# A shared root chain for two normalisations, the first tokens' normalisation on another engine, and four more unused products, in an RWKV and mixture-of-experts kernel

## The chip, the cores and the metric

The kernel runs on one core of one Trainium2 chip. A core has a matrix engine (TensorE, PE in the profile; its weight loads are listed as PEld), VectorE (DVE), ScalarE (ACT), GpSimd (POOL) and SyncE (SP), which issues most transfers. Each engine works through its own queue in order; semaphores tie the queues together. The metric is the device time of one execution in microseconds (us): the median of several runs.

## The reference, cut to what matters

Two blocks follow each other, each with a normalisation in front of it and a residual sum behind it. `x` has 4 sequences of 1024 tokens with 256 channels; everything is float32.

```python
def _layernorm(x, axis=-1, eps=1e-05):
    m = jnp.mean(x, axis=axis, keepdims=True)
    v = jnp.var(x, axis=axis, keepdims=True)
    return (x - m) / jnp.sqrt(v + eps)
...
# attention (RWKV), on the normalised tokens
xx = jnp.pad(x, ((0, 0), (1, 0), (0, 0)))[:, :Tv] - x
xk = x + xx * time_maa_k            # likewise xv, xr, xg
r, k, v = xr @ Wr.T, xk @ Wk.T, xv @ Wv.T
g = jax.nn.gelu(xg @ Wg.T, approximate=False)
def step(state, inp):
    rc, kc, vc = inp
    att = rc @ kc
    yc = att * Wmat @ vc + rc @ state * wb
    new_state = ws * state + kc * wk @ vc
    return (new_state, yc)
# y is normalised per head, then: out = yn * g @ Wo.T
...
# experts, on the tokens normalised again: 8 experts, the best 2 of each token, capacity 320
h1 = jnp.einsum('ebcm,emh->ebch', dispatch, w1)
h3 = jnp.einsum('ebcm,emh->ebch', dispatch, w3)
expert_out = jnp.einsum('ebch,ehm->ebcm', jax.nn.silu(h1) * h3, w2)
```

So every token is normalised twice: once ahead of the attention, and once, after the attention's output has been added, ahead of the experts.

## The kernel before, in words

**Blocks.** The 4096 tokens are worked in 16 blocks of 256 tokens (two tiles of 128), four to a sequence. The tokens lie in SBUF in rows of 512 tokens (`RT` = 4 tiles), so a row holds two blocks. For a block, `front` (L375) normalises the tokens (`xn`, by `normed`, L367), transposes them on PE (`trx`, L398), copies them out (`xT`, L401), takes the difference to the token before (`xx`, L405 on DVE for the first block, L407 on POOL for the others), mixes (`xm`, L413) and multiplies by the weights (`pc`, L423; `pt`, L464). `chunk` (L492) does the recurrence for one tile: scores `pa` (L502), their decay weights `aw` on DVE (L510), the outputs `y` (L524, L531) and the update of the state `pu` (L543) and `upd` (L550). `back` (L564) normalises per head (`sq`, `ys`, `var`, roots in `rsqrt`, `prs`), multiplies by the output weights (`po`, L610) and adds to the tokens (L615).

**Normalisation.** `norm_stats` (L329) works on one row: for each of its four tiles ACT sums the tokens (L347) and their squared deviations (L350), each followed by a read of the accumulator, and then DVE scales the variances (L354), takes their inverse roots by a bit trick and two steps of iteration (`rsqrt`, L308: ten small instructions, L317 to L325) and multiplies (L359). It is called with a key `a` ahead of the attention and with a key `f` in `logits` (L621) ahead of the experts. A call is a generator: each `yield` hands back to the loop, which decides when the next part is recorded. For the first 256 tokens the statistics are taken on DVE (`by_rows`, L337) and those of the other half of that row on ACT, behind the eight diagonals (L251, `last_diag`). `normed` is an ACT instruction for all tokens.

**Experts.** `logits` and `route` choose the experts and scatter the tokens to a buffer in HBM (L815) in five segments; `expert` (L850) loads weights and tokens, multiplies (`p`, L915, and `pw`, L936), and adds the results to the output by an indirect transfer (L943). These products fill PE between those of the attention.

**Order.** PE's order is written out by hand: the loop over blocks (L1091) goes through 15 stages, and in each it advances the parts listed for it (`f` and `fa` the fronts of later blocks, `c` the chunks, `bk` and `new` the backs, `st` the statistics), then `routing` by two steps, and then as many expert products as a credit allows (`RATES`). Experts of a segment may start `LAGS` stages after its routing is done. The queues of the other engines are set by a scheduler from the same record; `tc.issue_after(ins)` asks that what is recorded in its block comes behind `ins`. Until the change, the statistics of block n + 2 are taken in block n when n is even, and `f` statistics of a row one block after its second half.

**The start.** Ahead of the loop stand the first statistics, 18 products of ones with ones whose result nobody reads (`warm`, L1045), the statistics of the second half row, the first two fronts, and the decay tables: 16 instructions `wmat` (L257) on ACT, which need `lam`, which ACT computes (L222) and DVE clamps (L223).

```python
    with tc.issue_after(last["first_xn"]):
        decay_of_heads(0)
    with tc.issue_after(first_copy):
        decay_of_heads(1)
        decay_of_keys()
```

`first_xn` is the second of the two `xn` instructions of the first block (L386), kept in program order (L385).

Of the kernel before, what the change touches and what calls it, by code (L numbers as in the profile page):

```python
# [9 lines left out]
F32 = mybir.dt.float32  # L10
I32 = mybir.dt.int32
AF = mybir.ActivationFunctionType
ALU = mybir.AluOpType
# [4 lines left out]
P = 128  # L18
B, T, C = 4, 1024, 256
# [5 lines left out]
TPB = TB // P  # L25
BPS = T // TB
RB = 512
RT = RB // P
RPS = T // RB
# [11 lines left out]
AFTER = (0, 2, 3, 4)  # L41
# [5 lines left out]
LN_EPS = 1e-5  # L47
# [7 lines left out]

LAGS = (8, 5, 4, 4)

WARM = 18

SCORES = (0, 6)  # L60
MAGIC = 0x5F3759DF
ROOT = (64.0 / 9.0) ** 2
# [3 lines left out]
def rwkv_then_moe_kernel(  # L66
# [12 lines left out]
    nc = tc.nc  # L79
# [5 lines left out]
    sm = ctx.enter_context(tc.tile_pool(name="sm", bufs=1))  # L85
# [18 lines left out]
    xb = {}  # L104
# [203 lines left out]
    def rsqrt(v, n, nm):  # L308
# [17 lines left out]

        return y, (guess, lambda: step(9.0 / 64.0))

    def norm_stats(key, src, nm, t0=0, n=RT, behind=None, by_rows=False):  # L329

        ve = sm.tile([P, n], F32, tag=f"ve{n}", name=f"ve{nm}", bufs=2)
        nb = sm.tile([P, n], F32, tag=f"nb{n}", name=f"nb{nm}", bufs=2)
        if by_rows:
            st = sm.tile([P, n, 6], F32, tag="st", name=f"st{nm}", bufs=2)
            mv = sm.tile([P, n, 2], F32, tag="mv", name=f"mv{nm}", bufs=2)
            for t in range(n):
                nc.vector.bn_stats(st[:, t, :], src[:, t0 + t, :])  # L337
                nc.vector.bn_aggr(mv[:, t, :], st[:, t, :])
                yield
            mean, sign = mv[:, :, 0], -1.0  # L340
            nc.vector.tensor_scalar(ve, mv[:, :, 1], LN_EPS, ROOT, ALU.add, ALU.mult)
        else:

            mean, sign = sm.tile([P, n], F32, tag="mn", name=f"mn{nm}", bufs=2), 1.0
            for t in range(n):
                with tc.issue_after(behind) if behind else nullcontext():
                    nc.scalar.activation(  # L347
                        aside, src[:, t0 + t, :], AF.Copy, scale=-1.0 / C,
                        accum_out=mean[:, t:t + 1])
                nc.scalar.activation(  # L350
                    aside, src[:, t0 + t, :], AF.Square, bias=mean[:, t:t + 1],
                    accum_out=ve[:, t:t + 1])
                yield
            nc.vector.tensor_scalar(ve, ve, ROOT / C, LN_EPS * ROOT, ALU.mult, ALU.add)  # L354
        rs, parts = rsqrt(ve, n, nm)
        parts[0]()
        yield
        parts[1]()
        last["nb"] = nc.vector.scalar_tensor_tensor(  # L359
            nb, mean, sign, rs, ALU.mult, ALU.mult).ins  # L360
        stats[key] = rs, nb, t0

    stats = {}

    aside = const.tile([P, C], F32, tag="aside", name="aside")

    def normed(dst, src, key, t):  # L367
        rs, nb, t0 = stats[key]
        t -= t0
        return nc.scalar.activation(  # L370
            dst, src, AF.Identity, bias=nb[:, t:t + 1], scale=rs[:, t:t + 1])
# [249 lines left out]
    def logits(b, r):  # L621

        nm = f"{b}_{r}"
        nc.sync.dma_start(out=rows(out, b, r), in_=xb[b, r])
        yield from norm_stats(("f", b, r), xb[b, r], f"f{nm}")
        yield
        hs = a2.tile([P, RT, W], F32, tag="hs", name=f"hs{nm}")
        nc.gpsimd.iota(
            hs.bitcast(I32)[:, :, C:C + 1], pattern=[[P, RT], [0, 1]], base=b * T + r * RB,
            channel_multiplier=1)  # L630
        for t in range(RT):
            normed(hs[:, t, :C], xb[b, r][:, t, :], ("f", b, r), t)
            if t == TPB - 1:
                yield
        g = segment_of(b, r)
        t0 = r * RT - SEGMENTS[g][1]
        if t0 == 0:
            last["hs"] = []
            last["lg"] = sm.tile([P, SEGMENTS[g][2], E], F32, tag="lg", name=f"lg{g}", bufs=2)
        last["hs"].append(hs)  # L640
        yield from (None,) * (6 if g < AFTER[1] else 2)

        hTs = []
        for u in range(RT // TPB):
            pt = bank("m", f"trh{nm}_{u}")
            for cc in range(CC):
                for i in range(TPB):
                    nc.tensor.transpose(
                        pt[:, cc * TB + i * P:cc * TB + (i + 1) * P],
                        hs[:, u * TPB + i, cc * P:(cc + 1) * P], ident)  # L650
            hT = a1.tile([P, CC, TB], F32, tag="hT", name=f"hT{nm}_{u}", bufs=2)
            nc.scalar.copy(hT.rearrange("p cc i -> p (cc i)"), pt)
            hTs.append(hT)
            yield
        yield from (None,) * 3
        pl = bank("m", f"pl{nm}")
        for cc in range(CC):
            for t in range(RT):
                u, i = divmod(t, TPB)
                nc.tensor.matmul(  # L660
                    pl[32 * t:32 * t + 32, :P], gt[:, cc, :], hTs[u][:, cc, i * P:(i + 1) * P],
                    start=cc == 0, stop=cc == CC - 1, tile_position=(0, 32 * t),
                    skip_group_check=True,
                )
        lgT = sm.tile([P, P], F32, tag="lgT", name=f"lgT{nm}")
        nc.scalar.copy(lgT, pl[:, :P])
        yield from (None,) * 3
        pg = bank("m", f"plt{nm}")
        nc.tensor.transpose(pg[:, :P], lgT, ident)
        nc.scalar.copy(  # L670
            last["lg"][:, t0:t0 + RT, :],
            pg[:, :P].rearrange("p (t e) -> p t e", t=RT)[:, :, :E])
        yield from (None,) * 2
# [416 lines left out]
    with tc.manual_schedule(engines={ENG.PE}):  # L1090
        for n in range(NBLK):  # L1091
            b, blk = divmod(n, BPS)
            f, (fa, after) = f1, fronts(n + 2)
            st = iter(())
            if n + 2 < NBLK and n % RPS == 0:
                sb, sblk = divmod(n + 2, BPS)
                sr = sblk * TPB // RT
                st = norm_stats(("a", sb, sr, 0), xb[sb, sr], f"a{sb}_{sblk}", behind=last["xm"])
            if blk % RPS == 0 and b + 1 < B:
                load_x(b + 1, blk // RPS)  # L1100
            if blk == 0:
                last["state"] = None
            c = [chunk(b, blk, t, cur) for t in range(TPB)]
            new = back(b, blk, cur)
            for i, stage in enumerate((
                (c[0], st),
                (f, st),
                (c[0], st),
                (bk, st),
                (f, bk, st),  # L1110
                (c[0], st),
                (c[1], fa, st),
                (f,),
                (fa, bk),
                (c[1],),
                (f,),
                (bk,),
                (f,),
                (c[1], fa, new),
                (),  # L1120
            )):
                for part in stage:
                    steps(part)
                steps(routing, 2)
                clock.step += 1
                credit = min(credit + RATES[clock.turn], 4 * RATES[clock.turn])

                drain = i in SCORES
                while credit > 0 or drain:
                    drain = False  # L1130
                    cols = next(work, None)
                    if cols is None:
                        break
                    credit -= cols
            if n and n * TPB % RT == 0:
                pb, pblk = divmod(n - 1, BPS)
                routing = chain(routing, routed(pb, pblk * TPB // RT))
            cur, nxt, f1, bk = nxt, after, fa, new

        clock.mixed = True  # L1140
        for _ in bk:
            next(work, None)
        for _ in chain(routing, routed(B - 1, RPS - 1)):
            clock.step += 1
            if clock.step % 2:
                next(work, None)
        clock.mixed = False

        over = sm.tile([P, E + 1], F32, tag="over", name="over")
        nc.vector.tensor_scalar_add(  # L1150
            over[:, :E], last["base"], -float((TILES[B - 1] + SURE) * P))
        nc.vector.tensor_reduce(over[:, E:], last["base"], AX.X, ALU.max)
        nc.vector.tensor_scalar_add(over[:, E:], over[:, E:], -float(TILES[B] * P))
        last["over"] = sm.tile([P, E + 1], I32, tag="overi", name="overi")
        nc.vector.tensor_copy(last["over"], over)
        for _ in work:
            clock.step += 1
# [44 lines left out]
```

## Time and profile before

| what | value |
|---|---|
| median of 3 runs | 989.05 us (988.8 to 991.5) |
| the profiled execution | 978.46 us |
| its span, first to last instruction | 976.7 us |
| PE busy | 944.2 us (97%) |
| PEld busy | 749.7 us (77%) |
| DVE busy | 447.0 us (46%) |
| ACT busy | 320.1 us (33%) |
| POOL busy | 244.6 us (25%) |
| mean granted clock of PE | 0.988 |

In a line of the timeline the columns are: start in us from the span's start, length in us, engine, line of the kernel, operation, output <- inputs, shapes and number of instructions merged in the line; in brackets stands how long the engine had been idle before it and what ended that wait. `x4` on PE counts passes: a float32 product of 128 by 256 takes two. PEclk is the clock that PE was granted, as a share of full speed. A line of groups ends with busy time, mean length of one instruction in ns, and the idle time before.

### The profile page before, as it was taken

Reading aid. Unit: us, or ns where it says so; the run is one execution under the profiler, and the core shown is the slowest. Engines: PE = TensorE matmul, PEld = TensorE weight load, DVE = VectorE, ACT = ScalarE, POOL = GpSimd, SP = SyncE. Lnnn points to the kernel's source line nnn. Section 1 sums busy time; section 2 is a strip of 40 time slices with the busy share of each in tenths; the row PEclk is TensorE's granted clock in tenths of the full one; section 3 lists DMA queues with packets and bytes.
Section 4 is the critical chain, followed back from the end, with each engine's and each line's share of the span. In section 5 each row is a group of like instructions: output and inputs, shape, how many; then the busy total and the mean of one; then the engine's idle time right before and its main releaser. Section 6 shows DMA issues by size and latency. Waiting matters only on the chain. (4 is left out here: it accounts for less than half of the span.)

```text
span 976.7 us, 17096 instructions
## 1 busy us (share of the span) xinstructions
PE 944.2 (97%) x6754; PEld 749.7 (77%) x6754; DVE 447.0 (46%) x1303; ACT 320.1 (33%) x811; POOL 244.6 (25%) x265
## 2 busy tenths in 40 slices
PE   7989899999999999999999999999999999999995
PEld 6766678878787788888788778888866866767664
DVE  7888766656676634445443434322221222222221
ACT  8647544743654531524214124111111111111110
POOL 5321513312227212121452111541111110211111
PEclk9999999989999999999999999999999999999998
DMA  5997224514446444353465545785645234433421
GB/s 162 245 252 244 84 95 142 184 60 141 153 125 219 153 124 136 93 153 89 128 192 151 153 135 157 208 248 168 175 123 153 76 87 147 135 94 92 147 54 19
DMA packets 92073, 139.06 MB, mean 142 GB/s; under 512 B 5456, under 2 KB 73552, under 8 KB 91984
## 3 DMA queue, kind: packets, MB, share of 16 engines
q1 hardware_dynamic: 79120, 120.36, 39.2%
q0 software_dynamic: 12720, 17.47, 9.7%
q8 instruction: 58, 0.95, 0.4%
q14 instruction: 31, 0.25, 0.1%
q10 hardware_dynamic: 144, 0.02, 0.0%
HBM read 103.45 MB, written 34.39 MB: 141 GB/s over the span
## 5 line engine op out<-in xcount | busy, mean ns | idle before, releaser
L915 PE MATMUL p<-xeT,w 128*128 128x256 f32 (+2 forms) x1960 | 430.8, 374 | 2.8 <-DVE act L904 1.5
L915 PEld LDWEIGHTS p<-xeT,w 128*128 128x128 f32 x1960 | 328.4, 191 | 94.8 <-issue 10.5
L920 ACT ACTIVATE sl<-p 128x256 f32<-128x256 f32 (+2 forms) x245 | 91.2, 375 | 486.6 <-PE p L915 479.1
L904 DVE TENSOR_TENSOR act<-sl,p 128x256 f32<-128x256 f32 (+2 forms) x245 | 99.5, 408 | 284.2 <-ACT sl L920 168.4
L943 POOL DMA_INDIRECT y_out<-ye,xe x67 | 105.3, 1571 | 478.0 <-DVE ye L940 448.1
L936 PE MATMUL pw<-w,act 128*128 128x256 f32 x938 | 211.9, 381 | 0.3 <-DVE act L904 0.3
L936 PEld LDWEIGHTS pw<-w,act 128*128 128x128 f32 x938 | 174.9, 190 | 24.6 <-DVE act L904 1.0
L940 DVE TENSOR_SCALAR ye<-pw,xe 128x256 f32<-128x256 f32 x67 | 32.1, 483 | 138.6 <-PE pw L936 138.5
L510 DVE TENSOR_TENSOR aw<-pa,wmat 128x512 f32<-128x512 f32 x128 | 79.4, 683 | 11.4 <-PE pa L502 11.3
L815 POOL DMA_INDIRECT disp<-hs,is x64 | 63.7, 996 | 44.3 <-issue 15.4
L423 PE MATMUL pc<-xm,wa 128*128 128x256 f32 x264 | 67.1, 400 | 5.9 <-DVE aw L510 3.1
L423 PEld LDWEIGHTS pc<-xm,wa 128*128 128x128 f32 x264 | 50.2, 198 | 16.2 <-DVE aw L510 3.7
L413 DVE SCALAR_TENSOR_TENSOR xm<-xx,ch,xT 128x256 f32<-128x256 f32 x98 | 43.5, 479 | 8.5 <-PE pc L423 5.1
L502 PE MATMUL pa<-rT,kT 32*128 32x256 f32 x512 | 43.1, 410 | 2.0 <-DVE rbT L443 1.1
L531 PE MATMUL y<-aw,vpad 128*32 128x128 f32 x1024 | 40.5, 278 | 0.0
L347 ACT ACTIVATE aside<-x 128x256 f32<-128x256 f32 x62 | 25.7, 415 | 37.8 <-DVE x L615 37.0
L502 PEld LDWEIGHTS pa<-rT,kT 32*128 32x128 f32 x512 | 26.5, 187 | 11.2 <-issue 3.4
L610 PE MATMUL po<-wa,zT 128*128 128x256 f32 x128 | 30.7, 383 | 4.1 <-DVE zT L602 2.6
L531 PEld LDWEIGHTS y<-aw,vpad 128*32 128x32 f32 x1024 | 24.4, 109 | 12.2 <-issue 11.7
L464 PE MATMUL pt<-wa,xm 128*128 128x256 f32 x128 | 32.2, 397 | 0.9 <-DVE rbT L443 0.9
L407 POOL TENSOR_TENSOR xx<-xT 128x512 f32<-128x512 f32 x15 | 15.7, 1049 | 67.2 <-ACT xT L401 67.2
L610 PEld LDWEIGHTS po<-wa,zT 128*128 128x128 f32 x128 | 23.5, 190 | 7.9 <-ACT xT L393 2.8
(184 smaller groups left out, 797.3 us busy)
## 6 DMA issues: line engine op xcount, KB each, us to landing
w<-w_in SPq DMA_DIRECT2D x96, 896.0 KB, 6.4
disp<-empty SPq DMA_DIRECT2D x8, 795.0 KB, 15.4
disp<-empty SPq DMA_DIRECT2D x16, 265.0 KB, 9.5
xe<-disp SPq DMA_DIRECT2D x16, 265.0 KB, 2.9
xe<-disp SPq DMA_DIRECT2D x8, 530.0 KB
y_out<-x SPq DMA_DIRECT2D x8, 512.0 KB, 3.3
x<-x_in SPq DMA_DIRECT2D x7, 512.0 KB, 4.3
wa<-w_attn_in SPq DMA_DIRECT2D x5, 256.0 KB, 4.9
```

The source lines that it names most:

```text
L413: last["xm"] = nc.vector.scalar_tensor_tensor(xm[:, cc, :], xx[:, cc, :], maa(m, cc), xT[:, cc, 1:TB + 1], ALU.mult, ALU.add,).ins
L423: nc.tensor.matmul(pp[:, m * TB:(m + 1) * TB], wa[w][:, cc, m * P:(m + 1) * P], xm[:, cc, :], start=cc == 0, stop=cc == CC - 1,)
L502: nc.tensor.matmul(pa[g][:, cc * TB:(cc + 1) * TB], o.kT[rows32, cc, cols], o.rT[rows32, cc, :, cols], start=True, stop=True, tile_positio ...
L510: nc.vector.tensor_tensor(w.rearrange("p q i -> p (q i)"), pa[g], wmat[:, 4 * g:4 * g + 4, :].rearrange("p q i -> p (q i)"), ALU.mult,)
L531: nc.tensor.matmul(y[32 * g:32 * g + 32, :], o.vp[:, t, cc * 4 + g, q * 32:(q + 1) * 32], aw[g][:, cc * 2 + q, :], start=state is None and ...
L610: nc.tensor.matmul(po[:, t * C:(t + 1) * C], zT[:, cc, t * P:(t + 1) * P], wa[W_O][:, cc, :], start=cc == 0, stop=cc == CC - 1,)
L815: ins = nc.gpsimd.indirect_dma_start(out=disp[:, :], out_offset=bass.IndirectOffsetOnAxis(ap=idx_s[g][:, c, t:t + 1], axis=0), in_=last["h ...
L904: nc.vector.tensor_tensor(act, sl, p3[:, :w], ALU.mult)
L915: nc.tensor.matmul(pp[:, :w], wt[:, cc, f * P:(f + 1) * P], xeT[:, cc, lo:lo + w], start=cc == 0, stop=cc == CC - 1,)
L920: nc.scalar.activation(sl, p1[:, :w], AF.Silu)
L936: nc.tensor.matmul(po[:, :C], acts[f][:, i * P:(i + 1) * P], w2e[:, f, :], start=f == 0, stop=f == FC - 1,)
L943: ins = nc.gpsimd.indirect_dma_start(out=out[:, :], out_offset=bass.IndirectOffsetOnAxis(ap=xe.bitcast(I32)[:, t, C:C + 1], axis=0), in_=y ...
```

## The change

It has four parts. `WARM` goes from 18 to 22. The `xn` of the first block become DVE instructions. A new generator, `norm_pair`, takes the statistics of two rows together, the `f` row of blocks n - 3 and n - 2 and the `a` row of block n + 3, and runs one root chain over eight columns; it is used in blocks 3, 5, 7, 9 and 11, and the `a` statistics are taken in odd blocks instead of even ones (in block 0 and block 1 still by `norm_stats`). `logits` waits ten empty steps for a row whose statistics come from a pair, and two empty steps fewer behind its `hs`, for the first segments.

```diff
-WARM = 18
+WARM = 22
...
+    def norm_pair(keys, srcs, nm, behind):
+
+        n = 2 * RT
+        mean = sm.tile([P, n], F32, tag="mn8", name=f"mn{nm}", bufs=2)
+        ve = sm.tile([P, n], F32, tag="ve8", name=f"ve{nm}", bufs=2)
+        nb = sm.tile([P, n], F32, tag="nb8", name=f"nb{nm}", bufs=2)
+        for i, src in enumerate(srcs):
+            for t in range(RT):
+                o = i * RT + t
+                with tc.issue_after(behind) if i else nullcontext():
+                    nc.scalar.activation(
+                        aside, src[:, t, :], AF.Copy, scale=-1.0 / C,
+                        accum_out=mean[:, o:o + 1])
+                nc.scalar.activation(
+                    aside, src[:, t, :], AF.Square, bias=mean[:, o:o + 1],
+                    accum_out=ve[:, o:o + 1])
+                if t % 2:
+                    yield
+        nc.vector.tensor_scalar(ve, ve, ROOT / C, LN_EPS * ROOT, ALU.mult, ALU.add)
+        rs, parts = rsqrt(ve, n, nm)
+        parts[0]()
+        yield
+        parts[1]()
+        nc.vector.tensor_tensor(nb, mean, rs, ALU.mult)
+        for i, key in enumerate(keys):
+            sl = slice(i * RT, (i + 1) * RT)
+            stats[key] = rs[:, sl], nb[:, sl], 0
...
     def normed(dst, src, key, t):
         rs, nb, t0 = stats[key]
+        if key == ("a", 0, 0, 0):
+            return nc.vector.tensor_scalar(
+                dst, src, rs[:, t:t + 1], nb[:, t:t + 1], ALU.mult, ALU.add)
         t -= t0
         return nc.scalar.activation(
             dst, src, AF.Identity, bias=nb[:, t:t + 1], scale=rs[:, t:t + 1])
...
-        yield from norm_stats(("f", b, r), xb[b, r], f"f{nm}")
-        yield
+        if ("f", b, r) in paired:
+            yield from (None,) * 10
+        else:
+            yield from norm_stats(("f", b, r), xb[b, r], f"f{nm}")
+            yield
...
-        yield from (None,) * (6 if g < AFTER[1] else 2)
+        yield from (None,) * (4 if g < AFTER[1] else 2)
...
-            if n + 2 < NBLK and n % RPS == 0:
-                sb, sblk = divmod(n + 2, BPS)
+
+            m = n + 3 if n else 2
+            if m < NBLK and m % RPS == 0:
+                sb, sblk = divmod(m, BPS)
                 sr = sblk * TPB // RT
-                st = norm_stats(("a", sb, sr, 0), xb[sb, sr], f"a{sb}_{sblk}", behind=last["xm"])
+                key = "a", sb, sr, 0
+                if n > RPS:
+                    pb, pblk = divmod(n - 2, BPS)
+                    pr = pblk * TPB // RT
+                    paired.add(("f", pb, pr))
+                    st = norm_pair(
+                        (("f", pb, pr), key), (xb[pb, pr], xb[sb, sr]), f"p{sb}_{sblk}",
+                        last["xm"])
+                else:
+                    st = norm_stats(
+                        key, xb[sb, sr], f"a{sb}_{sblk}", behind=last["xm"])
```

## The prediction, made before the changed kernel ran

> **What bounds the kernel now.** I read the page first: which engine is busy, and how the 40 slices differ.
>
> ```profile
> span 976.7 us, 17096 instructions
> PE 944.2 (97%) x6754; PEld 749.7 (77%) x6754; DVE 447.0 (46%) x1303; ACT 320.1 (33%) x811; POOL 244.6 (25%) x265
> ```
>
> TensorE (PE) is busy for 944.2 of 976.7 us, so only its 32.5 us of idle time, and the speed of its clock, are open to a change that leaves the products alone. The timeline says where the idle time is: 5.0 us before 12.09, some 10 us after the last product, and 15.2 us in sixteen waits of 0.3 to 1.65 us, of which nine lie between 31 and 128 us (9.6 us together). After 330 us PE waits for hardly anything. The change touches the first two thirds of this list, so I read the head in the timeline of all engines.
>
> ```profile
> 3.41 2.43 ACT L251 ACTIVATE diag<-ident,ch 128x128 f32<-128x128 f32 x8
> ...
> 5.75 0.40 ACT L347 ACTIVATE aside<-x 128x256 f32<-128x256 f32 x1
> ...
> 6.45 0.17 DVE L223 TENSOR_SCALAR lam<-lam 128x16 f32<-128x16 f32 x1
> ...
> 8.35 1.09 ACT L370 ACTIVATE xn<-x,nba,rya 128x256 f32<-128x256 f32 x2 [0.30 <-DVE nba L359]
> ...
> 9.10 0.95 PE L398 MATMUL trx<-ident,xn 128*128 128x128 f32 x4 [1.79 <-ACT xn L370]
> ...
> 10.23 0.56 ACT L401 COPY xT<-trx 128x512 f32<-128x512 f32 x1
> ...
> 12.09 3.56 PE L423 MATMUL pc<-xm,wa 128*128 128x256 f32 x8 [2.04 <-DVE xm L413]
> ```
>
> The start is one chain: roots on VectorE (DVE), xn on ScalarE (ACT), transposes on PE, the copy on ACT, then the mix on DVE; at 12.09 the products begin and PE has no gap until 31. A delay here is therefore a delay of everything. Then the clock in half-microsecond stretches (length, busy time of PE, PEld, DVE, ACT, POOL, then PEclk).
>
> ```profile
> 11.50:12.00 0.50, 0.00 (x0) 0.00 (x0) 0.47 (x3) 0.50 (x3) 0.00 (x0) 0.87 1.10 361
> 12.00:12.50 0.50, 0.41 (x1) 0.41 (x2) 0.50 (x3) 0.50 (x3) 0.00 (x0) 0.50 1.11 358
> ```
>
> The first eight passes of real products run at half clock, until about 15.3. Last, a place in block 5 (numbered from 0) where a root chain stands in the way.
>
> ```profile
> 115.44 0.17 DVE L354 TENSOR_SCALAR vef<-vef 128x4 f32<-128x4 f32 x1 [1.53 <-ACT aside L350]
> ...
> 117.83 2.48 DVE L510 TENSOR_TENSOR aw<-pa,wmat 128x512 f32<-128x512 f32 x4
> ...
> 118.57 3.78 PE L423 MATMUL pc<-xm,wa 128*128 128x256 f32 x8 [1.65 <-DVE aw L510]
> ```
>
> DVE waits for statistics, runs eleven small steps, and only then aw, for which PE waits.
>
> **The head.** The built program of the change has three moves that the diff doesn't tell. The two xn on DVE stand behind the second half's root chain, not behind the first's. On ACT two decay products (L257) stand ahead of the eight diagonals, and the first of them waits for DVE's clamp of lam (L223). And three more decays stand between the statistics of the second half, which that root chain needs. ACT's queue is in order, so diagonals, statistics and the copy of xT queue behind that wait, and DVE's xn and PE's transposes wait for them.
>
> - lam is clamped by 6.62 in the trace, and a DVE result reached ACT in 0.04 (nb ended 8.31, xn began 8.35): the first decay starts at 6.66. Decays start 0.29 apart (8 take 2.44 at 0.39 each), so the diagonals start at 7.25, not 3.41: 3.84 late.
> - The statistics start at 5.75 + 3.84 = 9.59, take 2.30 as before (5.75 to 8.05) and three decays, 0.88: done at 12.77.
> - The second root chain took 8.37 to 10.69, 2.32 us; started at 12.80 it ends at 15.12.
> - Two xn on DVE: the nearest row of that size, L940, is 483 ns, but reads PSUM; the pair would be 0.9. The Trainium skill (VectorE: DVE Perf Modes, "The perf-mode tier table") gives fp32 tensor_scalar from SBUF two elements a cycle and tensor_tensor one; L698 (187 ns) beside 208 for two-tensor steps of its shape points the same way. By that rule the pair is 0.5. I take 0.5: done at 15.65.
> - From the last xn to the end of the transposes was 0.61 (9.44 to 10.05), and 0.18 to the copy: 16.44. ACT itself, after the statistics, has three decays (0.88) and two and a half pairs of block 2's statistics (1.16 a pair, 2.81): free at 16.46. The copy starts at about 16.5 for 10.23: **6.3 us late**. Bounds 5.8 (overlap of decays with accumulator reads) and 6.9 (xn at 0.9).
>
> From the copy to the products it was 1.86, so the products begin near 18.4. The four more products cost 4 x 0.25 (the last twelve passes, six products, took 1.50): they end at 8.3 for 7.3, hidden in the longer gap: nothing.
>
> Does the gap also cost clock? The Trainium skill (TensorE: Matmul & The Clock Gate, "Why this matters for your kernels") warns of idle gaps above about 3 us, after which the array runs at half clock. By it the old gaps (1.79 and 2.04) leave the clock full, the new one of 7 us does not, and the change would lose another 1.7 us (3.4 us at half speed). The row is against that: 0.50 at 12.00 already, after those two short gaps. The half-clock start is paid before and after: I add nothing, 1.7 at the most.
>
> **Relief in the following blocks.** Ten decays and part of the statistics are done in the wait. PE's waits near ACT's xn, 0.61 at 31.18 and 1.45 at 50.36, can shrink. Between 0 and 2.0: I take -0.8.
>
> **The joint chains.** Five pairs, each saving twelve DVE steps of 0.196 between starts: 2.3 us each, 11.5 of DVE. Only what PE waits for counts. The count of statistics on ACT stays. What is new: the joint step needs all eight tiles, and DVE's queue holds var and the root chain of the heads (and xeT's copy) behind it.
>
> - Block 5: upd and aw no longer wait for vef; 0.67 at 115.79 and 1.65 at 118.57 go, -2.3. But the second four tiles' statistics follow sq and ys (116.36), four pairs of 1.16: 121.0. xeT's copy stands behind the joint step, about 122.2; PE runs out at about 120.1: +2.1. Net -0.2.
> - Block 3: aw comes 2 us earlier where PE had other work. The joint step waits on ACT until about 80.3 (four pairs after ys, 75.68), var behind it (79.36 before), so rbT moves from 83.70 to 84.3; pt, now ahead of a transpose group (0.66), waits for rbT some 2.1 us for 0.86, and part comes back: +0.8.
> - Block 9: the joint step stands ahead of aw, ready near 253 for aw's 251.71, with expert products as partial cover: +0.5 (0 to 2). Blocks 7 and 11: expert products cover; 1.46 at 317.85 goes: -1.5.
>
> Together -0.4, bounds -4 and +6.
>
> **Clock spells.** PEclk was 0.88 and 0.77 in 110 to 130, and 0.68 in 200 to 210: 3.5 and 3.2 us of work lost. The first follows the waits that go, half a chance to vanish (-1.7); a new one in block 3 has a third (+1.2). Net -0.5, bounds -6.7 and +6.8.
>
> **Later routing.** Segments route one or two stages later, expert products with them; the early stages have PE idle of some 8%, 0.15 to 0.2 a stage: +0.3. DMA issue on SP only swaps neighbours: nothing.
>
> Sum: 6.3 - 0.8 - 0.4 - 0.5 + 0.3 = +4.9. On the profiled execution, 978.46 (span 976.7 and 1.76 around it), 983.4. The median of the runs is 989.05, 10.6 above the profiled one, so I add the difference there: 994.0.
>
> **Rivals.**
> - The late start is absorbed: the nine waits up to 128 us (9.6 us) give half back, since ACT's work was brought forward. +1.5: 990.5. Against: DVE is 88% busy there (68.84 of 78 us) and is late too. Chance 0.18.
> - Faster: the joint step never holds the queue, and with the waits at 115.79, 118.57 and 317.85 (3.8) both clock spells go (6.7). 6.3 - 0.8 - 3.8 - 6.7 = -5.0: 984.1. It decides at one point: whether the eighth tile's statistics are in before aw ends. By ACT's rows they are not in blocks 3 and 5. Chance 0.15.
> - Worse: the joint step holds aw or var in every pair and one clock spell more follows: 5 more, 999. Chance 0.13.
> - The first tokens are normalised right after the first roots, as the words say: xn done about 8.8, 0.6 sooner: 988.4. The built order excludes it unless the queue isn't what it shows: 0.02.
>
> The first account has 0.52. A measurement of this kernel tells apart about 0.3%, 986.1 to 992.0. Slower is the first account with its lower edge cut off (0.49) and the worse one (0.13): 0.62. Same: 0.22. Faster: 0.16. The range runs from 984.0 to 1000.0.
>
> **What would show it.** The timeline after: L257 ahead of L251 with an ACT wait until about 6.6; xn on DVE near 15.2; PE's first products near 18.4 at PEclk 0.50; no root chain ahead of aw in blocks 3 and 5, but a DVE wait for ACT's statistics behind it. Products beginning before 14 would make the prediction wrong, and so would PEclk at 1.00 throughout 100 to 210.

## The result, and the profile after

| | before | after |
|---|---|---|
| median | 988.92 us (6 runs, 987.86 to 991.95) | 995.95 us (6 runs, 994.53 to 999.0) |
| ratio, 95% interval | | 1.0066 (1.0052 to 1.0080) |
| the profiled execution | 978.46 us, span 976.7 | 999.0 us, span 997.2 |
| PE busy | 944.2 us | 955.4 us |
| mean granted clock | 0.988 | 0.985 |

The change costs 7.0 us by the medians, and its interval is clear of zero (5.1 to 7.9). The two profiled executions are 20.5 us apart. Most of the surplus belongs to neither kernel: the profiled execution of before is 10.6 us under the median of the runs shown with it, and two chips used below run the kernel before in 976.8 us, a third in 990.7. So I take the two profiles to be of chips of two kinds (the last section shows how they differ), and only what the two kernels do at the same instruction can be compared, not the lengths of their second halves.

The page of the kernel after:

```profile
span 997.2 us, 17051 instructions
PE 955.4 (96%) x6762; PEld 757.0 (76%) x6762; DVE 442.9 (44%) x1245; ACT 320.9 (32%) x809; POOL 246.2 (25%) x265
```

The start, in the timeline of all engines:

```profile
6.73 0.69 ACT L257 ACTIVATE wmat<-dist,lam 128x128 f32<-128x128 f32 x2 [3.11 <-DVE lam_c L226]
...
7.33 2.44 ACT L251 ACTIVATE diag<-ident,ch 128x128 f32<-128x128 f32 x8
...
12.46 0.17 DVE L382 TENSOR_SCALAR vea<-vea 128x2 f32<-128x2 f32 x1 [3.99 <-ACT aside L378]
...
14.70 0.73 DVE L399 TENSOR_SCALAR xn<-x,rya,nba 128x256 f32<-128x256 f32 x2
...
15.26 1.14 PE L430 MATMUL trx<-ident,xn 128*128 128x128 f32 x4 [5.99 <-DVE xn L399]
...
16.43 0.59 ACT L433 COPY xT<-trx 128x512 f32<-128x512 f32 x1 [0.36 <-PE trx L430]
```

The two decays stand ahead of the diagonals and wait 3.11 us for VectorE's clamp (the profile names the one of `lam_c`, L226, which follows that of `lam`); the diagonals follow at 7.33, the second half's statistics behind them, VectorE waits 3.99 us for these, and xn comes at 14.70. The transposes wait 5.99 us where they waited 1.79. The first products, in PE's timeline:

```profile
18.32 3.78 PE L455 MATMUL pc<-xm,wa 128*128 128x256 f32 x8 [1.92 <-DVE xm L445]
```

18.32 for 12.09: 6.23 us late. Their clock, in stretches of one microsecond (length, busy time of PE, PEld, DVE, ACT, POOL, then PEclk):

```profile
14.00:15.00 1.00, 0.00 (x0) 0.00 (x0) 0.86 (x6) 0.94 (x5) 0.00 (x0) 0.56 0.00 0
...
20.00:21.00 1.00, 1.00 (x3) 0.77 (x3) 1.00 (x5) 0.74 (x3) 0.00 (x0) 0.50 0.00 0
...
24.00:25.00 1.00, 1.00 (x5) 0.88 (x4) 1.00 (x3) 0.74 (x5) 1.00 (x1) 0.82 0.03 8
```

A stretch's mean tells where the clock changed in it: 0.56 is 0.12 us at full and 0.88 at half, so it fell at 14.12 and rose at 24.36. PE was at half clock for 6.0 us after its first product, where it had been for 3.2 before.

In block 5, VectorE's timeline:

```profile
124.13 0.23 DVE L582 TENSOR_TENSOR upd<-pu,par 128x64 f32<-128x64 f32 x1 [3.12 <-remote]
...
125.68 2.48 DVE L542 TENSOR_TENSOR aw<-pa,wmat 128x512 f32<-128x512 f32 x4 [1.33 <-PE pa L534]
...
129.65 0.17 DVE L347 TENSOR_SCALAR vep<-vep 128x8 f32<-128x8 f32 x1 [1.49 <-ACT aside L342]
```

No root chain stands between upd and aw any more; the joint one (L347) stands behind aw and waits for ScalarE there, as foretold.

### The profile page after: what moved, and what is told of

It is laid out like the page before. It is cut to its first block, busy times and chain, and to the rows that moved or that the text cites. A ratio compares the mean times of both kernels' runs of the same rounds, so it can differ in the third digit from the quotient of the medians.

```text
span 997.2 us, 17051 instructions
## 1 busy us (share of the span) xinstructions
PE 955.4 (96%) x6762; PEld 757.0 (76%) x6762; DVE 442.9 (44%) x1245; ACT 320.9 (32%) x809; POOL 246.2 (25%) x265
## 5 line engine op out<-in xcount | busy, mean ns | idle before, releaser
L534 PE MATMUL pa<-rT,kT 32*128 32x256 f32 x512 | 45.9, 417 | 3.6 <-DVE upd L582 3.5
L501 ACT COPY vpad<-pt 128x256 f32<-128x256 f32 x32 | 10.3, 374 | 63.6 <-PE pt L496 46.0
```

Of the source, the lines that this page charges most:

```text
L534: nc.tensor.matmul(pa[g][:, cc * TB:(cc + 1) * TB], o.kT[rows32, cc, cols], o.rT[rows32, cc, :, cols], start=True, stop=True, tile_positio ...
```

## The experiments

The theory is that of the prediction: the late start is the loss, and the joint chains are worth nothing that can be told. The rivals are that the joint step costs, that the following blocks absorb the start, and, within the start, that the clock costs more than the delay. Three chips were used; the kernel before took 990.69 us on the first (the four runs of the first group), 976.84 on the second and 976.78 on the third. Ratios are to the kernel before on the same chip.

**First group: the parts alone.**

One part undone:

```diff
-        if key == ("a", 0, 0, 0):
-            return nc.vector.tensor_scalar(
-                dst, src, rs[:, t:t + 1], nb[:, t:t + 1], ALU.mult, ALU.add)
```

> The changed kernel with one part undone: the first block's xn is ScalarE's again; the joint chains and the 22 warm products stay. Theory (the late start is the cause): ScalarE's queue begins with the eight diagonals again, the first products start at 12.1 (within 0.2), and the time falls back by about 6 to 7 us, to 988 to 990.5. Rival (the joint chains and the later routing are what costs): the start is early but the time stays at 993 to 996.

Measured: 991.01 us, 1.0003 (0.9990 to 1.0016). PE's timeline has the first products where they were before:

```profile
12.09 2.74 PE L452 MATMUL pc<-xm,wa 128*128 128x256 f32 x8 [2.04 <-DVE xm L442]
```

The loss is gone with this one edit.

One part alone, the same three lines added to the kernel before:

> The kernel before with one part added: the first block's xn on VectorE, nothing else. Theory (late start): two decays stand ahead of the diagonals as in the changed kernel, the first products start at 18.3 (18.0 to 18.8), and the time is 994.5 to 997. Rival (joint chains): the start is as late, but the slack of the following blocks takes most of it back, 989 to 991.

Measured: 995.04 us, 1.0048 (1.0032 to 1.0065), 4.4 us above before. ScalarE's queue and the first products are those of the change:

```profile
6.72 0.69 ACT L257 ACTIVATE wmat<-dist,lam 128x128 f32<-128x128 f32 x2 [3.13 <-DVE lam_c L226]
7.32 2.43 ACT L251 ACTIVATE diag<-ident,ch 128x128 f32<-128x128 f32 x8
...
18.29 3.50 PE L426 MATMUL pc<-xm,wa 128*128 128x256 f32 x8 [1.92 <-DVE xm L416]
```

The edit makes most of the loss by itself. It is 4.4 here and not 7.0; the intervals (3.2 to 6.4, and 5.1 to 7.9 of the whole change) overlap.

The joint chains alone (the first of these two with WARM at 18):

> The kernel before with one part added: the joint chains, with the moved statistics and logits; 18 warm products and xn on ScalarE. Theory: worth nothing that can be told, 987.5 to 990.5, and within 1 us of the run that differs from it only by four warm products. Rival (the joint step holds aw and var): 993 to 995.

Measured: 991.05 us, 1.0003 (0.9991 to 1.0015), and 0.04 from the kernel with four more warm products. Neither the joint step nor the warm products cost anything that can be told on this chip.

Then the change as its words say, with xn straight behind the first roots. Two ties of the program put xn late. `keep_in_program_order` ties it to the VectorE instruction traced just before it, which is the end of the second root chain. And `issue_after(last["first_xn"])` ties only instructions of first_xn's own engine: with first_xn on VectorE, ScalarE's decays lose their tie and drift ahead. Here xn is traced first, and the decays are tied to the copy of xT:

```diff
-    with tc.issue_after(first_nb):
-        steps(second, 2)
     f, cur = fronts(0)
-    steps(f, 4)
+    steps(f)
+    with tc.issue_after(last["first_xn"]):
+        steps(second)
+    steps(f, 2)
+    with tc.issue_after(last["xm"]):
+        steps(second)
+    with tc.issue_after(last["nb"]):
+        steps(f)
...
-    with tc.issue_after(last["first_xn"]):
-        decay_of_heads(0)
     with tc.issue_after(first_copy):
+        decay_of_heads(0)
+    with tc.issue_after(last["first_xn"]):
         decay_of_heads(1)
```

(xT's copy is also tied behind the second half's statistics, xx behind the first half of the second chain, and the second `first_xn` is block 1's.)

> The changed kernel as its words say: xn on VectorE straight behind the first roots, the second half's statistics behind it, ScalarE's decays behind the copy of xT. Theory: xn is done near 9.0, the copy near 10.0, the first products start between 11.5 and 12.3, and the time is 987.5 to 990. The prediction's rival of the words gives 988.4. If the cost lay in VectorE doing xn at all, it would stay above 993.

Measured: 992.04 us, 1.0014 (1.0002 to 1.0026); not the 987.5 to 990 expected. The start came as expected. Its timeline:

```profile
8.35 0.74 DVE L399 TENSOR_SCALAR xn<-x,rya,nba 128x256 f32<-128x256 f32 x2
...
11.65 1.99 PE L459 MATMUL pc<-xm,wa 128*128 128x256 f32 x8 [1.96 <-DVE xm L449]
...
34.53 3.39 PE L459 MATMUL pc<-xm_g,wa 128*128 128x256 f32 x8 [1.53 <-DVE aw L546]
```

So VectorE doing xn is no loss, and 0.44 us is won at the first product. It is lost again in the next blocks: PE waits 0.68 and 0.16 us for block 1's xn, 1.31 for block 2's at 32.01 and 1.53 for aw at 34.53, since ScalarE and VectorE now do the rest of the start's work there (eight decays and a tile's statistics stand on ScalarE between the copy of xT and block 1's xn at 13.69). The clock fell with these waits too: the eight passes at 34.53 took 3.39 us; the kernel with xn on ScalarE (the first run) had lost as much in the start. Block 3's transposes begin at 49.98, for 46.65 in that run. An early start isn't an early block 3.

**Second group: what in the late start costs.** The changed kernel itself comes first, as the measure:

> The changed kernel itself, on the chip of the next three, as their measure: 6 to 8 us above the kernel before, first products at 18.3. What differs between its profiles is execution, not program: theory says that the granted clock falls at another place of the start, but is at 0.50 for most of 14 to 24 us again, since PE stands for 6 us ahead of 15.3. If the fall were fixed to the instructions, it would be at 14.1 us and back at 24.4 us once more.

Measured: 980.58 us, 1.0042 (1.0026 to 1.0058), so 3.7 us above before, less than the 6 to 8 expected; first products at 18.27. The clock fell and rose elsewhere:

```profile
11.00:12.00 1.00, 0.00 (x0) 0.00 (x0) 0.00 (x0) 1.00 (x5) 0.00 (x0) 0.56 1.09 351
...
21.00:22.00 1.00, 1.00 (x7) 0.86 (x6) 0.66 (x2) 0.18 (x1) 0.00 (x0) 0.82 0.00 0
```

PE was at half clock from 11.12 to 21.36, where it had been from 14.12 to 24.36: the same length, 10.24 us, at another place, so its cover of real products was 3.1 us and not 6.0. The expectation of "most of 14 to 24" missed.

More warm products (`WARM = 44`), to keep PE awake:

> The changed kernel with 44 warm products instead of 22, so that PE works until about 15 us, when the first xn is there; the start stays late (products at 18.3 to 18.6). Theory (the long gap costs clock): the clock is full or falls once for 3.4 us at most, the first sixteen real passes take some 4 us in all instead of 6.5, and the time falls by 2 to 3 us from the changed kernel's. Rival (the prediction's step: the half-clock start is paid anyway): the time stays within 1 us of the changed kernel's.

Measured: 981.44 us, 1.0050 (1.0033 to 1.0066), no gain. But it doesn't decide: the products ended at 13.71, the gaps of 1.51 and 1.93 us around the transposes stayed, and the clock fell all the same, from 16.55 to 23.38.

The clamp first:

```diff
-    nc.vector.tensor_scalar(lam_c, lam_c, 1e3, 1e-32, ALU.min, ALU.max)
+    clamped = nc.vector.tensor_scalar(lam_c, lam_c, 1e3, 1e-32, ALU.min, ALU.max).ins
...
-    for _ in norm_stats(("a", 0, 0, 0), xb[0, 0], "a0_0", 0, TPB, by_rows=True):
-        pass
+    with tc.issue_after(clamped):
+        for _ in norm_stats(("a", 0, 0, 0), xb[0, 0], "a0_0", 0, TPB, by_rows=True):
+            pass
```

> The changed kernel with lam's clamp issued on VectorE ahead of the first statistics, so that ScalarE's first decays need not wait for it until 6.7: they can start when dist is there, 4.25. Everything else in the queues stays. Theory: ScalarE's diagonals, statistics and with them the second roots, xn and products come 2.4 to 2.5 earlier, products at 15.9 (15.7 to 16.3), and the time falls by 2 to 3 us from the changed kernel's. Rival (only the place of xn behind the second roots counts, ScalarE is not what it waits for): products stay at 18.3.

Measured: 978.38 us, 1.0015 (1.0008 to 1.0023), 2.2 below the changed kernel. The timeline of all engines:

```profile
4.24 0.69 ACT L257 ACTIVATE wmat<-dist,lam 128x128 f32<-128x128 f32 x2 [0.34 <-DVE lam_c L226]
4.83 2.43 ACT L251 ACTIVATE diag<-ident,ch 128x128 f32<-128x128 f32 x8
...
12.19 0.73 DVE L399 TENSOR_SCALAR xn<-x,rya,nba 128x256 f32<-128x256 f32 x2
...
16.06 3.40 PE L455 MATMUL pc<-xm,wa 128*128 128x256 f32 x8 [2.18 <-DVE xm L445]
```

The first decay starts 2.5 us sooner, and that is 2.5 us at xn, 2.2 at the first product and 2.2 in the time. The chain is what the prediction said it was.

The gaps of the start filled, with xn on ScalarE:

```diff
-WARM = 22
+WARM = 24
...
+        if b == 0 and blk == 0:
+            with tc.issue_after(turned):
+                for _ in range(7):
+                    filled = nc.tensor.matmul(warm[:, :P], ones, ones, start=True, stop=True)
```

> The changed kernel with xn back on ScalarE, 24 warm products, and seven more warm products between the first transposes and the first products, so that PE has hardly a gap from 1.2 to 12.1. Theory (gaps cost clock, in some executions): no stretch at 0.50 before 30 us, products at 12.1 to 12.4, mean granted clock of the runs higher by about 0.001 than with xn on ScalarE alone, and the time 0 to 1 us below that kernel's, at or a little under the kernel before. Rival (the gaps of 2 us are no cause of the fall): 0.50 is seen in the start as before.

Measured: 975.32 us, 0.9986 (0.9977 to 0.9995), the first below the kernel before, with no stretch at half clock before 30 us. But is it the filling or the joint chains?

**Third group: the clock apart from the delay, and the joint chains on a quicker chip.** The kernel before with the same filling:

> The kernel before with 24 instead of 18 warm products and seven more between the first transposes and the first products; separate chains, xn on ScalarE. Theory (the gain of the filled start is the start's clock alone, which is lost in some of the executions of before): 0.5 to 1 us below the kernel before, mean granted clock 0.001 to 0.0015 higher. Rival (the filled start needs the joint chains, which take the later clock spells away): no difference from before. If the joint chains were a burden, it would be the fastest of all, 2 us or more below before.

Measured: 976.40 us, 1.0000 (0.9989 to 1.0011). The mean granted clock of the runs rose (0.9926 for 0.9901), more than expected; the time didn't move by anything that can be told, though up to 1.1 us either way is not excluded. The start of block 2 tells where the gain goes, first with the filling, then in the second profile of before (the last run below):

```profile
29.95 0.33 PE L398 MATMUL trx<-ident,xn 128*128 128x128 f32 x1
31.59 0.55 PE L398 MATMUL trx<-ident,xn 128*128 128x128 f32 x3 [1.31 <-ACT xn L370]
```

```profile
31.25 0.70 PE L398 MATMUL trx<-ident,xn 128*128 128x128 f32 x4 [0.56 <-DVE upd L550]
```

Block 1 began 1.4 us sooner and block 2's first transpose 1.3; the other three wait for ScalarE's xn, which waited 1.15 us for VectorE's roots, and block 3 begins 0.1 us sooner.

The changed kernel with `WARM = 50` and the seven products:

> The changed kernel with 50 warm products, so that PE works until about 15.2, and seven more between the first transposes and the first products: the start is as late as in the changed kernel (products at 18.3 to 18.6), but PE has no gap ahead of it. Theory (of the cost of the change some 6 us are lateness that the following blocks partly absorb, and 1.5 to 3 us are clock): no stretch at 0.50 before 30 us, and 1.5 to 3 us below the changed kernel, so 1 to 4 above the kernel before. Rival (lateness is all): 4 to 6.5 us above the kernel before.

Measured: 980.08 us, 1.0034 (1.0023 to 1.0046). PE's timeline:

```profile
1.20 13.33 PE L1091 MATMUL warm<-ones 128*128 128x128 f32 x100 [1.20 <-POOL ones L143]
15.23 0.78 PE L430 MATMUL trx<-ident,xn 128*128 128x128 f32 x4 [0.70 <-DVE xn L399]
15.85 1.73 PE L436 MATMUL warm<-ones 128*128 128x128 f32 x14
17.93 1.99 PE L466 MATMUL pc<-xm,wa 128*128 128x256 f32 x8 [0.36 <-DVE xm L450]
```

Eight passes in 1.99 us where the changed kernel took 3.51 to 3.78, and still 3.3 us above before (2.2 to 4.5). That lies between the two accounts: it is within the theory's 1 to 4 above before, but only 0.4 to 0.8 us below the changed kernel (by the distances from before and by the ratios, of two chips), not 1.5 to 3. By the medians, then, most of the cost is lateness, as the rival had it; the intervals overlap and leave room for more clock in it, and the table below says more.

The joint chains alone once more, and the kernel before for a second profile:

> The kernel before with the joint chains alone, once more, on this chip: within 1.5 us of the kernel before, with a mean granted clock 0.001 to 0.002 higher, so that what it loses elsewhere is about what it gains there. If the joint chains are a gain that the other chip hid, 2 us below.

> The kernel before, for a second profile of it: its runs agree with the others of before; PE waits again near 31, 50, 115 and 118 us, of 0.6 to 1.7 us each; the clock falls in the start and near 110 to 130, at other microseconds than in the first profile or not at all. If the spells belonged to the instructions, they would be at 11.9 to 15.3 and 200 to 210 again.

Measured: the joint chains 975.01 us, 0.9983 (0.9972 to 0.9995), so 1.8 us below before on this chip (0.5 to 2.7), where they were level on the first. That is more than the 1.5 expected, and the mean granted clock is 0.0044 higher, not 0.001 to 0.002. Before: 976.49 us. It was at half clock from 12.45 to 15.86 in the start, from 118.3 to 121.7 and from 200.2 to 203.6; in its first profile from 11.9 to 15.3, 117.7 to 124.5 and 199.6 to 206.4. So the places recur, as the waits ahead of them do, and the length doesn't. Block 5, in PE's timeline of before, from 112 to 129:

```profile
115.84 1.13 PE L502 MATMUL pa<-rT,kT 32*128 32x256 f32 x10 [0.67 <-DVE upd L550]
118.59 3.50 PE L423 MATMUL pc<-xm,wa 128*128 128x256 f32 x8 [1.62 <-DVE aw L510]
...
127.57 1.16 PE L915 MATMUL p<-xeT,w 128*128 128x128 f32 x8 [1.80 <-DVE act L904]
```

And with the joint chains alone:

```profile
114.12 1.13 PE L531 MATMUL pa<-rT,kT 32*128 32x256 f32 x12 [0.76 <-ACT gT L519]
115.63 1.99 PE L452 MATMUL pc<-xm,wa 128*128 128x256 f32 x8 [0.38 <-DVE aw L539]
...
119.94 0.44 PE L916 MATMUL pe<-ident,xe 128*128 128x128 f32 x2 [1.95 <-DMA xe<-disp]
...
125.69 1.16 PE L947 MATMUL p<-xeT,w 128*128 128x128 f32 x8 [0.91 <-DVE act L936]
```

The two waits ahead of pc shrink from 2.29 to 1.14, and a new one of 1.95, for the experts' tokens, comes behind them; with one of 0.16 at 122.83 the waits of before are 4.25 in sum, and 4.00 after. What is won is the clock: 1.99 us for the eight passes of pc, 3.50 before.

**Where the time goes along the program.** Start of each block's transposes against the kernel before's second profile, in us (all four are of the two quicker chips):

| | block 0 | 1 | 3 | 5 | 7 | 9 | 12 | 15 | last product |
|---|---|---|---|---|---|---|---|---|---|
| joint chains alone | 0 | -1.4 | -1.0 | -2.4 | -5.1 | -7.4 | -5.6 | -4.0 | -2.3 |
| the change | +6.1 | +6.3 | +5.2 | +3.3 | +0.7 | -1.7 | +0.1 | +1.7 | +2.9 |
| the change, gaps filled | +6.1 | +4.4 | +4.7 | +2.8 | +0.7 | -1.7 | +0.2 | +2.0 | +3.2 |

The difference of the first two rows is what the late start does: 6.1 at block 0, 7.7 at block 1, 6.2 at block 3, 5.7 from block 5 to 12, 5.2 at the end. Row three tells how much of it is clock: 1.9 at block 1, 0.5 at blocks 3 and 5. (Behind that the filled kernel was at half clock from 121.27 to 124.69, which the other wasn't, so its row says no more of the start.) VectorE's `aw` of block 0 shows the give-back, filled and then not:

```profile
30.04 2.47 DVE L552 TENSOR_TENSOR aw<-pa,wmat 128x512 f32<-128x512 f32 x4
```

```profile
30.68 2.47 DVE L542 TENSOR_TENSOR aw<-pa,wmat 128x512 f32<-128x512 f32 x4
```

Of the 1.9 us that PE is ahead at block 1, VectorE is ahead by 0.6 here, and PE waits for it.

## Why the prediction was right, and where its terms were off

It foretold 994.0 and a loss; 995.95 came, within the range. By its steps:

- **The three moves and the late start, +6.3 at the copy of xT.** Right: 16.43 for 10.23 is 6.20. The diagonals began at 7.33 (foretold 7.25), the statistics were done at 12.46 (12.77: the decays lay partly beside the accumulator reads, which was the lower bound's reason), the pair of xn took 0.73 (0.5 was taken, an estimate from the Trainium skill's two elements a cycle, VectorE: DVE Perf Modes, "The perf-mode tier table", and 0.9 was the other bound; the trace lies between). PE's transposes then ended 0.97 behind the last xn, not 0.61, as the clock was at half. That these misses cancel is luck; the chain itself is the foretold one. Undoing the one edit restored the time, and 2.5 us off the clamp gave 2.2 back.
- **The four warm products, hidden.** Right: 0.04 us between the two kernels that differ by them.
- **Does the gap also cost clock? "I add nothing, 1.7 at the most."** Right in the sum, wrong in its reason. The reason was that the half-clock start "is paid before and after". It is paid before only in some executions: of eight profiles with the early start, the six whose gaps were left open show it three times (both of the kernel before, and the one with only xn put back) and three times not. With the late start and an open gap of 4.4 us or more it came four times of four. The price in the start is larger too, 1.9 us at block 1. But most of it isn't kept: by block 3 0.5 us of it are left, and the filled kernel is 0.8 us quicker by the ratios, whose intervals overlap. The prediction should have argued that the first blocks wait for VectorE, which it put at 88% busy in a stretch of 78 us, and so take clock loss back, as `aw` at 30.04 and 30.68 and block 2's xn show.
- **Relief in the following blocks, -0.8.** The lateness without the clock (row three less row one) falls from 6.1 at block 0 to 5.2 at block 5: -0.9.
- **The joint chains, -0.4, and clock spells, -0.5.** On the third chip -1.8 (-0.5 to -2.7), on the first +0.3 (-0.9 to +1.5). In block 5 "-2.3 + 2.1" was -1.15 + 0.90: both halves twice too large, the net right by luck. The second half isn't even the wait that was foretold: the joint step began at 120.65 (foretold 121.0), but PE waited 1.95 us ahead of it for a transfer, the experts' tokens from HBM, and not behind it for xeT's copy. In block 3 it began at 79.38 in a kernel that was 1.0 ahead by then, so at the 80.3 foretold, and rbT came 0.2 later by the same reckoning (83.01 for 83.75), not 0.6, since VectorE ran the joint steps in turn with those of var. PE had work meanwhile: the wait of pt (0.85) went, and one of 0.35 for hT came, -0.5 instead of +0.8. In block 11 the wait of 1.46 for aw became 0.29, but the one for act behind it grew from 0.29 to 1.40. The clock gain is real: 0.9945 for 0.9905 in the mean of the runs of those two kernels on the third chip. That it yields only 1.8 us, and that the lead of 7.4 us at block 9 shrinks to 2.3 at the last product, isn't explained by waits, which are as few in both. That the order in which expert products fill the blocks moved, as the term "later routing" (+0.3) had it in small, is a guess; no run tests it.
- **The sum.** +4.9 foretold. On the two quicker chips the late start is 5.2 to 5.7 by the table and the joint chains -1.8, so 3.4 to 3.9, against 3.7 measured; but the first of these is the change's profile less that of the joint chains, so the agreement is no check of its own, and xn alone was not run there. On the first chip xn alone gave 4.4 and the joint chains 0.3; the runs of the result gave 7.0. Which term makes the last 2 us there stays open. With 3.7 on one chip and 7.0 on another, that 994.0 came so near is in part luck.
- **The rivals.** "Absorbed" took half of the waits up to 128 us for slack; the table gives 0.9. "Faster" asked whether the eighth tile's statistics are in before aw ends; they weren't, VectorE waited 2.03 and 3.28 us for them in blocks 3 and 5, but behind aw, where it cost little. "As the words say" named 988.4, 0.6 below before; built for a trial it was 1.4 above.

No version is below both kernels on every chip. The joint chains with xn left on ScalarE are 1.5 us below before on the second chip (with filled gaps) and 1.8 on the third (alone), and level with it on the first.

## What to carry to other kernels

When an operation moves to another engine, look at what was tied to it: an order that held because two instructions shared a queue is gone, and what was held back by it may drift ahead of work that the critical chain needs. Price a late start by what the first blocks wait for; where they wait for a second engine that is late too, the delay stays, while clock lost in the same place is mostly given back. And taking 11.5 us of steps off an engine that isn't the bound was worth 1.8 us by the medians on one chip and nothing that can be told on another.

## What the hardware showed that was not expected

**The clock moves in steps of 3.41 us whose place differs by execution.** In the start PE was at half clock for 3.41 us (both profiles of before, and the change with xn back on ScalarE), 6.83 (the early clamp, the long warm-up) or 10.24 (both profiles of the change, and xn alone). The Trainium skill (TensorE: Matmul & The Clock Gate, "What's actually happening") says that the activity is judged in a free-running window of about 3.4 us, so that the change of clock differs from run to run; these rows agree. Read so, in the start of the fourteen profiles every window with PE busy 40% of the time or less (1.36 of 3.41 us ahead of 16.55 with the long warm-up) was followed by half clock, one with 77% (17.53 to 20.95 in the change) didn't bring full clock back, and one with 84% (15.52 to 18.93 with the early clamp) did. That would explain why the gaps of 2 us cost in some executions and those of 4.4 us and more in all: how much of a short gap falls in one window depends on where the windows lie. But busy time alone isn't the measure. Between 200 and 207 us in the first profile of before:

```profile
199.60:203.01 3.41, 3.41 (x20) 2.63 (x21) 2.07 (x5) 0.00 (x0) 0.31 (x1) 0.50 0.18 47
203.01:206.43 3.42, 3.42 (x11) 2.88 (x11) 0.81 (x2) 0.28 (x1) 0.00 (x0) 0.50 0.00 0
```

PE was busy all of the first window, 2.24 us of it with the scores `pa` (listed as 32*128, where the big products are 128*128), and full clock didn't come until a second one was over. What counts as busy is not shown.

**Two kinds of chip.** The joint chains alone are the same program in two runs, 986.8 us of span on the first chip and 972.3 on the third. Up to block 6's transposes at 103.9 us they agree within 0.05 us. Then, PE's timeline of the third chip and of the first:

```profile
112.42 0.31 PE L572 MATMUL pu<-vpad,kw 128*32 128x32 f32 x16
112.66 0.70 PE L531 MATMUL pa<-rT,kT 32*128 32x256 f32 x4
```

```profile
112.47 0.63 PE L572 MATMUL pu<-vpad,kw 128*32 128x32 f32 x12
113.58 0.23 PE L572 MATMUL pu<-vpad,kw 128*32 128x32 f32 x2 [0.48 <-issue]
114.32 0.23 PE L572 MATMUL pu<-vpad,kw 128*32 128x32 f32 x2 [0.51 <-issue]
...
117.06 2.07 PE L531 MATMUL pa<-rT,kT 32*128 32x256 f32 x10 [1.28 <-DVE upd L579]
119.08 3.78 PE L452 MATMUL pc<-xm,wa 128*128 128x256 f32 x8
```

On the slower chip PE stands twice for half a microsecond and waits for nothing that the profile shows, VectorE's upd comes late, and the clock falls behind it: 3.3 us at one place. The change's profile has the same stops, at 120.94 and 121.67, and others near 318 us. All five profiles with long spans (987 to 997 us: the change and the first group) have such stops behind 20 us, 3.8 to 5.6 us in each, and none of the nine with short ones (972 to 980) has any. With them block 5's relief is gone before it counts, which fits that the joint chains gained nothing on that chip. What the stops are the trace doesn't say.
